# A list scheduler that makes its plan 48 times and keeps one, in a four-layer attention kernel

## The chip, the cores and the metric

One Trainium2 chip, one of its cores. The metric is device time in microseconds (us), lower is better. The engines are PE (matrix multiply; its weight loads are shown as PEld), DVE (vector), ACT (scalar and activation functions), POOL (GpSimd) and SP, whose queue issues the DMAs here. They run side by side, each in the order of its own instruction list, and wait for one another through semaphores.

## The reference

The input is x, 128 sequences of 64 tokens with 128 features, a context of the same shape and one conditioning vector per sequence, all float32. Four transformer layers follow one another. Cut to its blocks, in order:

```
L0: x = x + attn(adaln(x), adaln(ctx)) @ Wp
L1: x = x + gate * self_attn(adaln(x));  x = x + cross_attn(ln(x), ln(ctx))
    x = x + gate * gelu_mlp(adaln(x))
L2: x = x + gate * self_attn(adaln(x))
    x = x + gate * topk_cross_attn(adaln(x), ctx)      # softmax over the 16 largest of 64 scores
    x = x + gate * swiglu_mlp(adaln(x))
L3: x = x + gate * self_attn(adaln(x));  x = x + cross_attn(ln(x), ctx)
    x = x + gate * gelu_mlp(adaln(x))
```

Every attention has 16 heads of 8 features over 64 keys. There are seven attentions and three MLPs.

## The kernel before

**Tiling.** The 128 sequences are cut into 16 chunks of 8 sequences (512 tokens). A chunk goes through all four layers on its own. Eight lanes hold one chunk each; a lane whose list of work has become short takes the next chunk. So up to eight chunks, in different layers, are interleaved on the engines, and one fills the waits of another.

**The planner.** No order is written by hand. While the kernel is being built, on the host, `lane()` describes a chunk as operations: `op(engine, cost, outs, ins, give, latency)`. An operation is a group of instructions (for example the 64 matmuls that weigh the values of four sequences) with a hand-set weight in nanoseconds for the time it holds its engine, and a latency until its result can be used. `Plan.run` is a list scheduler: at each step it looks at the first 80 operations of each lane, asks `Plan.start` for the earliest time by the weights at which each could start (engine free, inputs ready, 150 ns for a hop between engines, 1300 ns for another activation table, a free tile, and for runs of small matmuls a term for the fetching of instructions, `late`), and gives out the one that can start first. `give_out` writes its instructions, and `in_turn` ties them to the previous ones of the same engine, so the chip executes each engine's list in the order of the plan. The weights set only this order: on the chip an instruction runs as soon as it is at the head of its engine's list and its inputs are there.

**Filling matmuls.** Where the plan finds that PE will stand idle for over 1000 ns before an operation that takes a fresh PSUM tile, `warm` (L1010 to L1018) puts dummy matmuls there into that tile, with columns for half the planned gap (`idle / 2`, at 1.7 ns a column). They are real instructions on the chip (L1017 in the profile). Their number of columns is thus a record of where the plan had gaps on PE, and how long.

**What the change touches.** In an attention, one operation makes the queries (PE, L586), ACT writes them to SBUF (L589), and then four DMAs spread them over a mask-shaped tile `qbd` whose other rows are zero, so that one matmul serves four heads. This transfer is the operation on SP at L595:

```
def spread():
    for j in range(4):
        nc.sync.dma_start(out=qbd()[j::4, j, :], in_=qT()[j::4, :])

op(SP, 1600, [qbd], [qT], spread, 2500)
```

The scores (L638, in the top-k attention L668) read `qbd`. ACT takes the exponentials (L649), PE weighs the values (L769), DVE divides (L778, L781), PE transposes (L816), ACT copies (L820), PE projects (L866). In the top-k attention, DVE finds the 16 largest scores of each row (L706, L708, L710, L721), and POOL masks (L736), ahead of transposes on PE (L744). A layer norm is DVE statistics (L530, L542), one POOL power (L545), DVE scaling (L550) and a PE transpose (L518). The gates of the residuals come from DRAM by DMAs on the same SP queue (L830). After the last chunk a small check (L1051 to L1061) decides whether a second, slow version of the whole network, which is also in the program, has to run; it does not run with these inputs.

Of the kernel before, what the change touches and what calls it, by code (L numbers as in the profile page):

```python
# [2 lines left out]

# [6 lines left out]
F32 = mybir.dt.float32  # L10
# [4 lines left out]
P = 128  # L15
# [4 lines left out]
T = CB * S  # L20
# [5 lines left out]
MLP = 512  # L26
LANES = 8
NJ = MLP // P
NSOME = 30
NQBD, NPROB, NVAL = 3, 8, 4  # L30
SCALE = 1.0 / math.sqrt(HD)
# [64 lines left out]
PE, DVE, ACT, POOL, SP = "PE", "DVE", "ACT", "POOL", "SP"  # L96


class Planned:


    def __init__(self, make, kind, turn):
        self.make, self.kind, self.turn = make, kind, turn
        self.real, self.writer, self.readers, self.ops, self.end = None, None, [], [], 0.0

    def __call__(self):
        if self.real is None:
# [4 lines left out]
class Operation:  # L112
    def __init__(self, engine, cost, latency, tiles, needs, give, bulk, table, small, within):
        self.engine, self.cost, self.latency = engine, cost, latency
        self.tiles, self.needs, self.give, self.bulk = tiles, needs, give, bulk
        self.table, self.small, self.within = table, small, within
        self.end = None


class Plan:  # L120

# [7 lines left out]
    BLOCK = 256  # L131
    FETCH = 3400.0

    def __init__(self, tc, slots, warm):
        self.tc, self.last, self.warm = tc, {}, warm
        self.size = slots
        self.free = {kind: [(0.0, k) for k in range(n)] for kind, n in slots.items()}
        self.made, self.next_turn = {}, {}
        self.engine_free = dict.fromkeys((PE, DVE, ACT, POOL, SP), 0.0)
        self.ops = None  # L140
        self.table = None
        self.small, self.blocks = 0, [(k, -self.FETCH) for k in range(0, self.BLOCK, 32)]
# [9 lines left out]

    def kept(self, real):
        t = Planned(None, None, None)
        t.real = real
        return t

    def op(self, engine, cost, outs, ins, give, latency=0.0, bulk=False, table=None, small=0, within=False):
        tiles = list(dict.fromkeys([*outs, *ins]))
        needs = {}  # L160
        for t in tiles:
            if t.writer is not None:
                needs[t.writer] = True
        for t in outs:
            needs.update(dict.fromkeys(t.readers))
        o = Operation(engine, cost, latency, tiles, needs, give, bulk, table, small, within)
        for t in outs:
            t.writer, t.readers = o, []
        for t in ins:
            if t not in outs:  # L170
                t.readers.append(o)
        for t in tiles:
            t.ops.append(o)
        self.ops.append(o)

    def start(self, o, first=True):
        at = self.engine_free[o.engine]
        if o.table not in (None, self.table):
            at += self.SWITCH
        if o.engine == PE and bool(o.small) != bool(self.small):  # L180
            at += self.SHAPE
        for d in o.needs:
            if d.end is None:
                return None
            at = max(at, d.end + (self.HOP if d.engine != o.engine else 0.0))
        want = {}
        for t in o.tiles:
            if t.real is None:
                want.setdefault(t.kind, []).append(t)
        o.want = want  # L190
        if want:
            if o.engine == PE:

                seen = {o}
                for t in o.tiles:
                    if t.kind in self.PSUM and t.real is None and not all(self.led(p, seen, want) for p in t.ops):
                        return None
            for kind, tiles in want.items():
                if len(self.free[kind]) < len(tiles) + (0 if first or kind != "some" else self.SPARE):
                    return None  # L200
                if tiles[0].turn is not None:
                    first = self.next_turn.get(kind, 0)
                    if sorted(t.turn for t in tiles) != list(range(first, first + len(tiles))):
                        return None
            for t in o.tiles:
                if t.real is None:
                    at = max(at, sorted(self.free[t.kind])[want[t.kind].index(t)][0])
        if o.small:
            at += self.late(o, at)
        return at  # L210
# [19 lines left out]
    def led(self, p, seen, want):  # L230

        if p.end is not None or p in seen:
            return True
        if not all(self.led(d, seen, want) for d in p.needs):
            return False
        seen.add(p)
        for t in p.tiles:
            if t.real is None and t not in want.setdefault(t.kind, []):
                want[t.kind].append(t)
        return True  # L240

    def give_out(self, o, at):
        idle, fresh = at - self.engine_free[o.engine], None
        for t in [t for tiles in o.want.values() for t in tiles]:
            if t.real is None:
                slots = self.free[t.kind]
                empty, t.slot = min(slots)
                slots.remove(min(slots))
                if o.engine == PE and t.kind in self.PSUM:
                    idle, fresh = min(idle, at - empty), fresh or t  # L250
                if t.turn is not None:
                    self.next_turn[t.kind] = t.turn + 1
                t()
        if fresh and idle > self.IDLE:
            self.in_turn(lambda: self.warm(fresh(), idle / 2))
        self.in_turn(o.give)
        self.table = o.table or self.table
        if o.engine == PE:
            self.small = o.small
            if o.small:  # L260
                self.late(o, at, True)
        self.engine_free[o.engine] = at + o.cost
        o.end = at + o.cost + o.latency
        for t in o.tiles:
            t.end = max(t.end, o.end)
            if t.kind is not None and all(p.end is not None for p in t.ops):
                self.free[t.kind].append((t.end + self.HOP, t.slot))
# [13 lines left out]

    def run(self, lanes, count):

        todo = [[] for _ in lanes]
        chunk = 0
        while True:
            for n, write in enumerate(lanes):
                if len(todo[n]) <= self.AHEAD and chunk < count:
                    self.ops = []
                    write(chunk)  # L290
                    todo[n] += [(chunk, o) for o in self.ops]
                    chunk += 1
            best = None
            oldest = min((c for ops in todo for c, _ in ops), default=None)
            for n, ops in enumerate(todo):
                for i, (c, o) in enumerate(ops[: self.WINDOW]):
                    at = self.start(o, c == oldest or o.within)
                    if at is not None and (best is None or (at, o.bulk, i, c) < best[0]):
                        best = (at, o.bulk, i, c), n, i, o
            if best is None:  # L300
                assert not any(todo), "no operation can start"
                return
            (at, *_), n, i, o = best
            del todo[n][i]
            self.give_out(o, at)
# [3 lines left out]
def kernel(ctx: ExitStack, tc: tile.TileContext, ins: dict, out: bass.AP, nchunk: int = NCHUNK):  # L309
# [33 lines left out]
    with tc.tile_pool(name="condw", bufs=1) as condw:  # L343
        cw = {}
        for key, wname, _, kinds in CONDS:
            n = len(kinds.split())
# [124 lines left out]
    def lane(n, plan, work, safe, acc, vblocks, queries, pool):  # L471
# [100 lines left out]
        def attention(hq, hkv, wq, bq, wk, wv, topk=False):  # L572
# [19 lines left out]
                for j in range(4):  # L592
                    nc.sync.dma_start(out=qbd()[j::4, j, :], in_=qT()[j::4, :])

            op(SP, 1600, [qbd], [qT], spread, 2500)  # L595


            pv = mm("pv")
# [410 lines left out]
    def network(lanes, safe, acc=None):  # L1009
        def warm(tile, ns):  # L1010
# [4 lines left out]
            while columns > 0:  # L1015
# [1 line left out]
                nc.tensor.matmul(flat[:, :n], lhsT=ident, rhs=W["L1_xcond_W_mlp1"][:, :n], start=True, stop=True)  # L1017
                columns -= n  # L1018

        plan = Plan(tc, {"mm": 3, "ps": 2, "po": 1, "qbd": 1 if safe else NQBD, "prob": 2 if safe else NPROB,  # L1020
                          "values": 1 if safe else NVAL, "some": 10 if safe else NSOME}, warm)
        with tc.tile_pool(name=f"work{int(safe)}", bufs=1) as work:


            vblocks = []
            for k in range(plan.size["values"]):
                v = work.tile([P, NPAIR, NH, 2, HW], F32, tag=f"vbuf{k}", name=f"vbuf{k}", bufs=1)
                nc.gpsimd.memset(v, 0.0)
                for b in range(2):
# [1 line left out]
                vblocks.append(v)  # L1031

            queries = []
            for k in range(plan.size["qbd"]):
                q = work.tile([P, 4, T], F32, tag=f"qbd{k}", name=f"qbd{k}", bufs=1)
                nc.gpsimd.memset(q, 0.0)
                queries.append(q)
            pool = [work.tile([P, T], F32, tag=f"some{k}", name=f"some{k}", bufs=1) for k in range(plan.size["some"])]
            plan.run([lane(n, plan, work, safe, acc, vblocks, queries, pool) for n in range(min(lanes, nchunk))], nchunk)
        return plan  # L1040

    acc = [const.tile([P, m], F32, name=k) for k, m in (("recsum", 4 * NH), ("fitting", 4 * NH), ("taken", 8))]
    fits = const.tile([P, 4 * NH], F32, name="fits")
# [45 lines left out]
```

## Time and profile before

| what | value |
|---|---|
| runs shown | 2002.7 us median (1995.64, 2002.7, 2008.0) |
| the profiled execution | 2011.3 us, its span 2009.5 us |
| PE, PEld, DVE, ACT, POOL busy, share of the span | 89%, 64%, 74%, 60%, 49% |
| mean granted PE clock | 0.977 of full speed |
| filling matmuls (L1017) on PE | 74.55 us in 220 records |
| weighing of the values (L769) on PE | 28672 matmuls, 314.2 us |
| exponentials (L649) on ACT | 384, 1025 ns each |
| `qbd` transfers (L593) on SP | 448, 64 KB each, 592 ns median issue, 1.9 us from issue to landing |
| gate transfers (L830) on SP | 448, 128 KB each, 616 ns median issue, 3.3 us to landing |

A busy time is the sum over an engine's instructions. A matmul of float32 data shows as two records. In the view by waits, each idle stretch of an engine is put down to what ended it; "issue" is idle time that ended without any release the profile shows. In the view by stretches of time, a column gives the busy us of each engine, the number of its instructions, and the clock granted to PE.

### The profile page before, as it was taken

What the parts mean: (1) busy time and instruction counts of PE and PEld (TensorE: products, weight loads), DVE (VectorE), ACT (ScalarE), POOL (GpSimd) and SP (SyncE); (2) the same over time, 40 slices, a digit from 0 to 9 for tenths busy, and PEclk for the clock granted to TensorE, in tenths of its full rate; (3) what the DMA queues carried; (4) which work ended last, traced back from release to release, by engine and by line L of the source; (5) the groups of instructions that cost most, each with busy time, mean ns of one, the idle gap of its engine ahead of it and who ended that gap; (6) DMA issues with size and microseconds to landing.
All of it is one profiled execution on the core that took longest, in us unless ns stands there. A gap on an engine that the chain in (4) does not pass through costs nothing. (4 is left out here: it accounts for less than half of the span.)

```text
span 2009.5 us, 104010 instructions
## 1 busy us (share of the span) xinstructions
PE 1791.5 (89%) x45345; PEld 1280.5 (64%) x45345; DVE 1488.3 (74%) x6641; ACT 1203.1 (60%) x1737; POOL 993.5 (49%) x1125
## 2 busy tenths in 40 slices
PE   4799889899899889999999988999898999888987
PEld 3466666666676666676676666676666666565564
DVE  3854546899989999787966496979588955989632
ACT  0356566675666657666665676677566665664443
POOL 2853534456455555555555355455454545444422
PEclk7899999999999999999999999999989999999999
DMA  5311222122122211222222222122112122121211
GB/s 173 88 51 51 66 62 66 54 58 73 57 68 63 69 51 53 69 83 66 65 67 66 64 73 63 51 68 66 56 55 61 45 71 61 56 65 31 66 31 35
DMA packets 203669, 127.51 MB, mean 63 GB/s; under 512 B 16764, under 2 KB 187972, under 8 KB 203204
## 3 DMA queue, kind: packets, MB, share of 16 engines
q1 hardware_dynamic: 196868, 115.44, 19.1%
q8 instruction: 359, 5.88, 1.2%
q10 hardware_dynamic: 6336, 5.31, 0.9%
q14 instruction: 106, 0.87, 0.2%
HBM read 86.22 MB, written 5.11 MB: 45 GB/s over the span
## 5 line engine op out<-in xcount | busy, mean ns | idle before, releaser
L649 ACT ACTIVATE prob<-ps 128x1024 f32<-128x1024 f32 x384 | 380.4, 1025 | 162.6 <-PE ps L638 161.7
L769 PEld LDWEIGHTS po<-vbuf,prob 128*32 128x32 f32 x28672 | 283.7, 110 | 140.4 <-issue 104.1
L769 PE MATMUL po<-vbuf,prob 128*32 128x18 f32 x28672 | 314.2, 187 | 54.0 <-issue 52.3
L545 POOL TENSOR_TENSOR rstd<-rstd,minus_half 128x4 f32<-128x4 f32 x192 | 200.3, 1046 | 154.9 <-DVE rstd L542 149.0
L736 POOL TENSOR_TENSOR some<-some,some 128x512 f32<-128x512 f32 x128 | 165.1, 1292 | 203.6 <-ACT some L728 199.7
L550 DVE TENSOR_SCALAR some<-x,parts,rstd 128x128 f32<-128x128 f32 x640 | 231.7, 425 | 44.6 <-POOL rstd L545 42.9
L638 PE MATMUL ps<-qbd,some 32*64 32x256 f32 x6144 | 238.0, 391 | 23.1 <-issue 18.1
L854 POOL TENSOR_TENSOR x<-x,some 128x512 f32<-128x512 f32 x112 | 143.9, 1286 | 208.5 <-DVE some L853 191.0
L708 DVE MATCH_REPLACE8 some<-m,some 128x64 f32<-128x64 f32 x1024 | 206.3, 209 | 0.0
L845 POOL TENSOR_TENSOR x<-x,some 128x512 f32<-128x512 f32 x112 | 145.6, 1300 | 104.9 <-DVE some L550 63.0
L778 DVE RECIPROCAL rec<-po 128x32 f32<-128x32 f32 x224 | 78.5, 350 | 154.6 <-PE po L769 149.0
L611 ACT COPY vbuf<-pv 64x512 f32<-64x512 f32 x224 | 139.0, 621 | 89.1 <-PE pv L604 86.9
L638 PEld LDWEIGHTS ps<-qbd,some 32*64 32x64 f32 x6144 | 122.8, 132 | 102.2 <-issue 66.4
L706 DVE MAX8 m<-some 128x8 f32<-128x64 f32 x1024 | 173.9, 211 | 9.8 <-ACT some L686 9.8
L710 DVE MAX8 m<-some 128x8 f32<-128x64 f32 x1024 | 176.8, 214 | 0.0
L853 DVE TENSOR_TENSOR some<-py,some 128x512 f32<-128x512 f32 x112 | 76.9, 687 | 121.0 <-PE py L879 50.0
L518 PE MATMUL pn<-ident,some 128*128 128x128 f32 x768 | 129.3, 286 | 31.4 <-issue 14.7
L582 ACT COPY some<-pk 128x512 f32<-128x512 f32 x112 | 66.0, 589 | 127.4 <-PE pk L580 120.4
L518 PEld LDWEIGHTS pn<-ident,some 128*128 128x128 f32 x768 | 90.0, 142 | 80.8 <-issue 32.3
L560 POOL TENSOR_TENSOR some<-some,mod_L 128x512 f32<-128x512 f32 x112 | 118.5, 1060 | 44.5 <-DVE some L559 40.0
L530 DVE BATCH_NORM_STATS2 parts<-x 128x6 f32<-128x256 f32 x320 | 121.0, 420 | 24.8 <-POOL x L854 16.1
L800 POOL TENSOR_SCALAR fits<-rec 128x64 f32<-128x64 f32 x112 | 42.7, 382 | 172.2 <-DVE rec L778 167.6
(219 smaller groups left out, 3632.7 us busy)
## 6 DMA issues: line engine op xcount, KB each, us to landing
some<-gates_dram SPq DMA_DIRECT2D x448, 128.0 KB, 3.3
qbd<-some SPq DMA_DIRECT2D x448, 64.0 KB, 1.9
some<-in_ctx_dram SPq DMA_DIRECT2D x64, 256.0 KB, 4.1
x<-in_x_dram SPq DMA_DIRECT2D x16, 256.0 KB, 4.6
out_dram<-x SPq DMA_DIRECT2D x16, 256.0 KB, 2.3
row<-in_biases_dram SPq DMA_DIRECT2D x17, 64.0 KB, 3.0
gates_dram<-gates SPq DMA_DIRECT2D x1, 896.0 KB
cw_L<-in_L_xcond_w_ada_dram ACTq DMA_DIRECT2D x1, 576.0 KB, 6.3
```

The source lines that it names most:

```text
L518: nc.tensor.transpose(p()[:, t * P : (t + 1) * P], x()[:, t, :], ident)
L545: op(POOL, 1070, [rstd], [rstd], lambda: nc.gpsimd.tensor_tensor(rstd(), rstd(), minus_half, ALU.pow))
L550: nc.vector.tensor_scalar(xn()[:, t, :], x()[:, t, :], mv()[:, t, 1:2], rstd()[:, t : t + 1], ALU.subtract, ALU.mult)
L638: nc.tensor.matmul(pscs[g // 2]()[b * S : (b + 1) * S, g % 2, u].rearrange("p (h q) -> p h q", h=4), lhsT=kT()[rows, cols], rhs=qbd()[rows ...
L649: op(ACT, 1020, [pr], [psc], lambda pr=pr, psc=psc: nc.scalar.activation(pr().rearrange("p g u h q -> p (g u h q)"), psc().rearrange("p g ...
L706: nc.vector.max(m1()[:, j, :], ex()[:, j, :])
L708: nc.vector.match_replace(w()[:, j, :], m1()[:, j, :], ex()[:, j, :], GONE)
L710: nc.vector.max(m2()[:, j, :], w()[:, j, :])
L736: op(POOL, 1310, [ex], [ex, w], lambda ex=ex, w=w: nc.gpsimd.tensor_tensor(ex(), ex(), w(), ALU.mult))
L769: nc.tensor.matmul(po()[32 * part : 32 * part + 32, h].rearrange("p b w -> p (b w)"), lhsT=prs[gp]()[:, gi, u, j, 32 * half : 32 * half + 32],
L845: op(POOL, 1310, [x], [x, g], lambda: nc.gpsimd.tensor_tensor(x(), x(), g(), ALU.add), bulk=True)
L854: op(POOL, 1310, [x], [x, y], lambda: nc.gpsimd.tensor_tensor(x(), x(), y(), ALU.add))
```

## The change

The planner is made able to run without writing instructions (`tc` is None), and somewhat faster by bookkeeping (`missing`, `ready`, `taken`). Each operation's weight is multiplied by a random factor between 0.99 and 1.01 from a seeded generator. The plan is made for seeds 0 to 47; the seed whose plan ends first by its own (varied) weights is then carried out. A plan that gets stuck counts as endless. The second, slow network takes seed 0. Separately, the weight of the mask transfer on SP goes from 1600 to 2900 ns, its latency stays 2500. No operation is added, removed or changed.

```diff
+TRIES = 48
 class Operation:
+        self.end, self.after = None, []
+        self.missing = sum(d.end is None for d in needs)
+        self.ready = 0.0
+        for d in needs:
+            d.after.append(self)
+            if d.end is not None:
+                self.ready = max(self.ready, d.end + (Plan.HOP if d.engine != engine else 0.0))
...
 class Plan:
-    def __init__(self, tc, slots, warm):
-        self.tc, self.last, self.warm = tc, {}, warm
+    def __init__(self, tc, slots, warm, seed):
+        self.tc, self.last, self.warm, self.random = tc, {}, warm, random.Random(seed)
...
-        o = Operation(engine, cost, latency, tiles, needs, give, bulk, table, small, within)
+        o = Operation(engine, cost * self.random.uniform(0.99, 1.01), latency, tiles, needs, give, bulk, table, small, within)
...
-        for d in o.needs:
-            if d.end is None:
-                return None
-            at = max(at, d.end + (self.HOP if d.engine != o.engine else 0.0))
+        at = max(at, o.ready)
...
-                t()
-        if fresh and idle > self.IDLE:
-            self.in_turn(lambda: self.warm(fresh(), idle / 2))
-        self.in_turn(o.give)
+                if self.tc is not None:
+                    t()
+        if self.tc is not None:
+            if fresh and idle > self.IDLE:
+                self.in_turn(lambda: self.warm(fresh(), idle / 2))
+            self.in_turn(o.give)
...
+                    if o.missing or best and max(o.ready, self.engine_free[o.engine]) > best[0][0]:
+                        continue
                     at = self.start(o, c == oldest or o.within)
...
-                assert not any(todo), "no operation can start"
-                return
+                return math.inf if any(todo) else max(self.engine_free.values())
...
-            op(SP, 1600, [qbd], [qT], spread, 2500)
+            op(SP, 2900, [qbd], [qT], spread, 2500)
...
+        def planned(seed, tc=None, work=None, *tiles):
+            plan = Plan(tc, slots, warm, seed)
+            tiles = tiles or (None, None, None)
+            return plan.run([lane(n, plan, work, safe, acc, *tiles) for n in range(min(lanes, nchunk))], nchunk)
+
+        seed = 0 if safe else min(range(TRIES), key=planned)
...
-            plan.run([lane(n, plan, work, safe, acc, vblocks, queries, pool) for n in range(min(lanes, nchunk))], nchunk)
-        return plan
+            assert planned(seed, tc, work, vblocks, queries, pool) < math.inf
```

More of the change, by code (lines that the diff above doesn't have):

```diff
@@ L1 @@
 import math
+import random
 from contextlib import ExitStack
@@ L104, in __init__ @@
         self.real, self.writer, self.readers, self.ops, self.end = None, None, [], [], 0.0
+        self.taken = False
     def __call__(self):
@@ L116, in __init__ @@
         self.table, self.small, self.within = table, small, within
-        self.end = None
+        self.end, self.after = None, []
[5 more added lines that the diff above has]
+                self.ready = max(self.ready, d.end + (Plan.HOP if d.engine != engine else 0.0))
 class Plan:
@@ L154, in kept @@
         t = Planned(None, None, None)
-        t.real = real
+        t.real, t.taken = real, True
         return t
@@ L181, in start @@
             at += self.SHAPE
-        for d in o.needs:
-            if d.end is None:
-                return None
-            at = max(at, d.end + (self.HOP if d.engine != o.engine else 0.0))
+        at = max(at, o.ready)
         want = {}
         for t in o.tiles:
-            if t.real is None:
+            if not t.taken:
                 want.setdefault(t.kind, []).append(t)
@@ L195, in start @@
                 for t in o.tiles:
-                    if t.kind in self.PSUM and t.real is None and not all(self.led(p, seen, want) for p in t.ops):
+                    if t.kind in self.PSUM and not t.taken and not all(self.led(p, seen, want) for p in t.ops):
                         return None
@@ L205, in start @@
             for t in o.tiles:
-                if t.real is None:
+                if not t.taken:
                     at = max(at, sorted(self.free[t.kind])[want[t.kind].index(t)][0])
@@ L237, in led @@
         for t in p.tiles:
-            if t.real is None and t not in want.setdefault(t.kind, []):
+            if not t.taken and t not in want.setdefault(t.kind, []):
                 want[t.kind].append(t)
@@ L244, in give_out @@
         for t in [t for tiles in o.want.values() for t in tiles]:
-            if t.real is None:
+            if not t.taken:
+                t.taken = True
                 slots = self.free[t.kind]
@@ L263, in give_out @@
         o.end = at + o.cost + o.latency
+        for d in o.after:
+            d.missing -= 1
+            d.ready = max(d.ready, o.end + (self.HOP if d.engine != o.engine else 0.0))
         for t in o.tiles:
@@ L293, in run @@
             best = None
-            oldest = min((c for ops in todo for c, _ in ops), default=None)
+            oldest = min((ops[0][0] for ops in todo if ops), default=None)
             for n, ops in enumerate(todo):
                 for i, (c, o) in enumerate(ops[: self.WINDOW]):
+                    if o.missing or best and max(o.ready, self.engine_free[o.engine]) > best[0][0]:
+                        continue
                     at = self.start(o, c == oldest or o.within)
@@ L1018, in warm @@
                 columns -= n
-        plan = Plan(tc, {"mm": 3, "ps": 2, "po": 1, "qbd": 1 if safe else NQBD, "prob": 2 if safe else NPROB,
-                          "values": 1 if safe else NVAL, "some": 10 if safe else NSOME}, warm)
+        slots = {"mm": 3, "ps": 2, "po": 1, "qbd": 1 if safe else NQBD, "prob": 2 if safe else NPROB,
+                 "values": 1 if safe else NVAL, "some": 10 if safe else NSOME}
+        def planned(seed, tc=None, work=None, *tiles):
[3 more added lines that the diff above has]
+        seed = 0 if safe else min(range(TRIES), key=planned)
         with tc.tile_pool(name=f"work{int(safe)}", bufs=1) as work:
             vblocks = []
-            for k in range(plan.size["values"]):
+            for k in range(slots["values"]):
                 v = work.tile([P, NPAIR, NH, 2, HW], F32, tag=f"vbuf{k}", name=f"vbuf{k}", bufs=1)
@@ L1033, in network @@
             queries = []
-            for k in range(plan.size["qbd"]):
+            for k in range(slots["qbd"]):
                 q = work.tile([P, 4, T], F32, tag=f"qbd{k}", name=f"qbd{k}", bufs=1)
@@ L1037, in network @@
                 queries.append(q)
-            pool = [work.tile([P, T], F32, tag=f"some{k}", name=f"some{k}", bufs=1) for k in range(plan.size["some"])]
-            plan.run([lane(n, plan, work, safe, acc, vblocks, queries, pool) for n in range(min(lanes, nchunk))], nchunk)
-        return plan
+            pool = [work.tile([P, T], F32, tag=f"some{k}", name=f"some{k}", bufs=1) for k in range(slots["some"])]
+            assert planned(seed, tc, work, vblocks, queries, pool) < math.inf
     acc = [const.tile([P, m], F32, name=k) for k, m in (("recsum", 4 * NH), ("fitting", 4 * NH), ("taken", 8))]
```

## The prediction

> **What bounds the kernel now.** I read the page first, then the view by stretches of time for the whole kernel, the same view for the filling matmuls alone (L1017), PE's waits, and three stretches closer.
>
> ```profile
> span 2009.5 us, 104010 instructions
> PE 1791.5 (89%) x45345; PEld 1280.5 (64%) x45345; DVE 1488.3 (74%) x6641; ACT 1203.1 (60%) x1737; POOL 993.5 (49%) x1125
> PE   4799889899899889999999988999898999888987
> ...
> DVE  3854546899989999787966496979588955989632
> ```
>
> PE is near full from the third slice to the last, DVE is full only in some slices. By stages (all engines, then L1017 alone):
>
> ```profile
> 0.00:100.00 100.00, 60.40 (x723) 40.41 (x723) 60.31 (x176) 20.86 (x29) 51.73 (x72) 0.83 0.45 131
> 100.00:1800.00 1700.00, 1555.45 (x41420) 1125.06 (x41421) 1308.80 (x5898) 1091.80 (x1577) 869.12 (x973) 0.99 0.21 62
> 1800.00:2009.50 209.50, 175.62 (x3204) 115.07 (x3204) 119.17 (x569) 90.41 (x132) 72.64 (x80) 0.97 0.14 40
> ```
>
> ```profile
> 0.00:100.00 100.00, 13.00 (x26) 5.72 (x26) 0.83 0.45 131
> 100.00:1800.00 1700.00, 23.76 (x86) 15.31 (x86) 0.99 0.21 62
> 1800.00:2009.50 209.50, 37.79 (x108) 18.93 (x108) 0.97 0.14 40
> ```
>
> First number after the length: PE busy. PE's own work is 1791.47 - 74.55 = 1716.9 us, and the change leaves every operation as it is, so only the rest of the span can move: 292.6 us of filling matmuls and idle PE. By stage that is 100 - 60.40 + 13.00 = 52.6 us at the start, 1700 - 1555.45 + 23.76 = 168.3 us in the middle and 209.5 - 175.62 + 37.79 = 71.7 us at the end.
>
> What the middle's idle time waits for on PE:
>
> ```profile
> PE po L769 <- issue: 51.8, 53, 2.1
> PE ps L638 <- issue: 18.1, 22, 2.0
> PE ps L668 <- issue: 10.7, 11, 2.3
> PE ppt L744 <- POOL some L736: 5.1, 6, 2.0
> PE pn L518 <- DVE some L550: 4.3, 7, 0.9
> ```
>
> Of the 144.55 us idle there, all "issue" waits come to 91 us, nearly all ahead of or inside the runs of small matmuls; waits for other engines are about 53.5 us in many small pieces. Three stretches show what the lanes' phases do to DVE:
>
> ```profile
> 400.00:700.00 300.00, 275.04 (x7212) 201.10 (x7215) 277.55 (x1402) 194.59 (x297) 165.68 (x179) 0.98 0.22 64
> 1600.00:1700.00 100.00, 93.96 (x2271) 67.45 (x2260) 51.54 (x136) 60.35 (x83) 50.14 (x62) 1.00 0.22 66
> 1790.00:1850.00 60.00, 50.82 (x1022) 34.13 (x1022) 58.07 (x367) 30.76 (x51) 25.43 (x27) 1.00 0.14 42
> ```
>
> Third busy number: DVE. It is 93% busy at 400 to 700, half idle at 1600 to 1700, and then 97% busy at 1790 to 1850, where the last top-k attentions come together and PE stops for them. After about 1940 one chunk is alone and PE waits at each link of its chain:
>
> ```profile
> 1986.66 2.54 PE L1017 MATMUL pn<-w_L_xcond_W_mlp,ident 128*128 128x512 f32 x6
> 1990.10 1.10 PE L518 MATMUL pn<-ident,some 128*128 128x128 f32 x4 [0.90 <-DVE some L550]
> ```
>
> So PE bounds the middle, DVE the stretch before the end, and one chunk's latency the end.
>
> **The change, part by part.** It changes only the order on each engine and the filling matmuls. I compared the two instruction lists. PE's are the same for some 70 matmuls and then differ nearly everywhere: this is another plan, not a retouched one.
>
> *Filling matmuls as a map of the plan's gaps.* Splitting the lists after 400 and 21,808 real matmuls (of 23,493 in the list; the second split is where the trace stands at 1800 us), the filling columns are 5,507 / 10,560 / 18,303 before and 5,697 / 12,392 / 13,169 after. Sums 34,370 and 31,258. So the new plan has shorter gaps at the end (-5,134), longer ones in the middle (+1,832), and the same start (+190).
>
> Price at the end: with all lost time put on the columns, 71.7 / 18.303 = 3.92 us per thousand; with the matmuls alone, 37.79 / 18.303 = 2.06. Ends of the range: -20.1 and -10.6 us. I take -20.1, since the two lines above show that filler and idle share each gap.
>
> Price in the middle: the matmuls alone 23.76 / 10.56 = 2.25 us per thousand, with the waits for engines (23.76 + 53.5) / 10.56 = 7.32. Ends: +4.1 and +13.4 us. No row tells which, as many waits lie where no filler stands; I take the half, +8.8.
>
> Start: 13.00 / 5.507 = 2.36 per thousand gives +0.4 (all lost time there: +1.8). I take +0.4.
>
> *Instruction waits of small matmuls (91 us).* They depend on how the runs follow each other. Of 223 steps from one run of L769 to the next, those with under 7 us of PE work from start to start are 153 before and 156 after (rows times their durations), so I take 0; ends -9 and +9, a tenth of the 91.
>
> On this the Trainium skill ("Runtime: NRT & Kernel Launch", Instruction fetch mechanics) says that instructions are fetched ahead in blocks of 256 and that the fetch is hidden, because a sequencer issues more slowly than the blocks arrive. The 53 waits ahead of L769 here speak against that for these runs, though the trace doesn't name their cause; by the rule the order could neither gain nor lose here, and the ends of this term would be 0.
>
> *Top-k work on DVE.* One of the 64 top-k groups costs DVE (206.3 + 176.8 + 173.9 + 83.6 + 96.2) / 64 = 11.5 us (rows L708, L710, L706, L708 loads, L721). In the last 3,000 real matmuls the new list has 8 groups against 12: 46 us of DVE work moved out of the 97% stretch into the earlier one where DVE is half idle. That is the reason behind the shorter gaps at the end, priced already. From 4,000 to 8,000 real matmuls (about 370 to 710 us) it has 20 groups against 16: 46 us more where DVE has 7% to spare. It is part of the longer gaps in the middle, and the rival below.
>
> *Table loads.* 70 against 72 on ACT before the end of the network, 1.28 us each, 2.6 us of an engine that is 60% busy: 0. If PE's cover were gone (the end), at most -2.6.
>
> *The mask's weight.* On the chip four issues take 2.4 to 2.5 us of SP in most cases, and a transfer lands 1.9 us after its issue, so qbd is complete about 1.8 + 1.9 = 3.7 us after the first issue (estimate from these rows). By the weights: 4.1 us before, 5.4 after; SP is held 1.6 before, 2.9 after. So the hold on SP is nearer than it was, the time to the result farther. In the middle PE waits for a qbd DMA once, 0.8 us, so little can be gained. The larger time makes the plan put other work ahead of the scores; the chip is not made to wait by that, except that in the last chunk alone two attentions could be put 1.3 us late: ends -0.8 and +2.6, I take 0. Behind a mask on SP stand mostly gate transfers (mask then gate 78 times before, 80 after), for which DVE L853 waits 46.9 us in all and POOL L845 27.1; both are waits off PE, so 0, unless they fall in the DVE-full stretch.
>
> *Sum.* -20.1 + 8.8 + 0.4 + 0 + 0 + 0 = -10.9 us. The profiled execution goes from 2011.3 (2009.5 of span and 1.8 around it) to 2000.4. It lay 8.6 us above the median shown; against the median, 2002.7 - 10.9 = 1991.8, so 1992 us. Within 1% means 1983 to 2023, about what a measurement can tell from no change.
>
> **Rivals.**
>
> *Slower: the top-k jam in the first wave.* The 46 us of added DVE work at 370 to 710 us meet about 25 us of idle DVE (7.5% of 340). 46 - 25 = 21 us don't fit, and PE, which needs the masked scores, ends the stretch 21 us later. If the end gives nothing back, because the last chunk's chain and not DVE sets it, the time is 2002.7 + 21 = 2024. For it: fillers between 4,000 and 6,000 real matmuls rise from 1,652 to 3,113 columns. Against: by 8,000 both lists have given out 23 groups, and other DVE work can move out. It decides against the change once the stretch grows by more than the end shrinks, 10.6 to 20.1 us.
>
> *Faster than 1%.* The plan's gain at the end (-20.1) comes whole, the middle costs only its fillers (+4.1) and the instruction waits fall by 9: -24.6, so 1978. For it: all gaps shorten together when the plan as a whole ends earlier. Against: 91 us of the waits are not the plan's to remove.
>
> *Nothing: the choice by weights doesn't carry over.* Variations of one per cent are smaller than the errors of the weights (the mask's own was off by half), so the chosen order is a random draw on the chip: 2003, plus or minus ten. Against: the fillers' places agree with the chip's gaps in the trace (108 of 220 records after 1800 us). The change not doing what it says is out: the lists differ and have fewer fillers.
>
> **How the numbers follow.** My forecast (small gain, 1983 to 2000) 0.35; nothing (1993 to 2013) 0.22; faster than 1% 0.26; the jam beyond 1% 0.17. Hence faster by over 1%: 0.26; within 1%: 0.35 + 0.22 = 0.57; slower by over 1%: 0.17. Range: low 1966, which is 1978 less the 7 us by which the lowest run lay under the median and less 5 for the unknown ends; high 2018, where most of the jam's case is left out. The likeliest case alone: 1983 to 2000.
>
> **What would show it.** In the changed profile: fillers (L1017) near 27 us after the end stage's start, 28 in the middle, 13 at the start; the stage after 21,808 real matmuls near 190 us instead of 209.5; DVE not full in the last stretch before one chunk is alone; the stretch from 370 to 710 us as long as before, to 9 us; "issue" waits of PE's small matmuls still near 91 us; PE's own work 1717 us. Wrong would be: a DVE at 97% or more around 400 to 750 us with PE waiting for L736 or L550; an end as long as before with fewer fillers but more idle; or issue waits that differ by more than 9 us.

## The result and the profile after

| | runs | median | lowest to highest |
|---|---|---|---|
| before | 18 | 2000.61 us | 1992.18 to 2010.68 |
| changed | 18 | 1989.4 us | 1982.45 to 1999.74 |

The ratio is 0.9948, 95% interval 0.9929 to 0.9966: 0.5% faster, clear of noise and within the 1%. The profiled execution of the changed kernel took 1987.86 us, its span 1986.1. In the changed kernel's code the line numbers are 16 higher: L1017 has become L1033, L769 is L785, L638 is L654, L853 is L869.

The page after, the same lines as before:

```profile
span 1986.1 us, 103877 instructions
PE 1784.4 (90%) x45327; PEld 1276.6 (64%) x45327; DVE 1495.9 (75%) x6641; ACT 1199.0 (60%) x1735; POOL 997.1 (50%) x1125
PE   4799899989988989999989899899999898988987
...
DVE  3854445999999999975777966499959977998632
```

PE still bounds. DVE is now at 90% or more in one long stretch, from the eighth to the seventeenth slice, and the two slices at 5 that stood ahead of the end (33 and 34) are now at 7. To set stage against stage, the cuts have to lie at the same real matmul (400 and 21,808 of the list), not at the same time. In the trace these stand at 104.8 and 1797.6 us before (the rows count records, two for a matmul of float32 data, so the 28672 of L769 in the table ahead are records too):

```profile
0.00:104.80 104.80, 65.20 (x763) 42.95 (x764) 65.08 (x184) 22.75 (x32) 55.95 (x76) 0.82 0.43 125
104.80:1797.60 1692.80, 1548.25 (x41251) 1120.36 (x41250) 1301.75 (x5879) 1087.51 (x1572) 864.90 (x970) 0.99 0.21 63
1797.60:2009.50 211.90, 178.02 (x3336) 117.23 (x3334) 121.45 (x581) 92.81 (x136) 72.64 (x80) 0.97 0.14 41
```

and at 103.4 and 1791.0 us after (all engines, then the fillers, L1033, alone):

```profile
0.00:103.40 103.40, 64.88 (x767) 42.71 (x771) 63.39 (x183) 22.70 (x31) 54.90 (x75) 0.85 0.44 126
103.40:1791.00 1687.60, 1553.96 (x41245) 1118.94 (x41248) 1333.02 (x6026) 1086.56 (x1579) 871.74 (x972) 0.99 0.21 62
1791.00:1986.10 195.10, 165.56 (x3330) 114.97 (x3326) 99.46 (x434) 89.74 (x127) 70.45 (x80) 0.95 0.15 46
```

```profile
0.00:103.40 103.40, 14.40 (x28) 6.20 (x28) 0.85 0.44 126
103.40:1791.00 1687.60, 27.65 (x94) 15.76 (x94) 0.99 0.21 62
1791.00:1986.10 195.10, 28.20 (x80) 14.68 (x80) 0.95 0.15 46
```

Lost time of PE is length less busy plus fillers. The fillers of the kernel before keep their 13.00, 23.76 and 37.79 us with these cuts.

| stage | lost before | lost after | difference | forecast |
|---|---|---|---|---|
| start | 52.6 | 52.9 | +0.3 | +0.4 |
| middle | 168.3 | 161.3 | -7.0 | +8.8 (4.1 to 13.4) |
| end | 71.7 | 57.7 | -14.0 | -20.1 (-20.1 to -10.6) |
| PE's own work | 1716.9 | 1714.2 | -2.8 | 0 |

The two profiles differ by 23.4 us, the medians by 11.2. The three chips of the experiments below ran the kernel before at medians of 2011, 2013 and 2014 us; its profile, at 2011.3, is like those, and the changed kernel's, at 1987.9, is like the result's runs. So about half of the 23.4 us isn't the change's, and nothing tells in which stages it lies. The -2.8 us in PE's own work say nothing of the change either: a second profile of the kernel before (at the end of the experiments) has 1714.0. Below, each kernel is compared with the kernel before on its own chip.

What PE's idle time waited for has changed as well. In the middle stage of the changed kernel the longest rows of the view by waits are:

```profile
PE po L785 <- issue: 52.4, 55, 2.2
PE ps L654 <- issue: 9.0, 12, 1.6
PE ppt L760 <- POOL some L752: 7.3, 9, 1.9
```

and in the end stage these, first before, then after:

```profile
PE ppt L744 <- POOL some L736: 6.4, 6, 1.9
PE po L769 <- issue: 0.5, 1, 0.5
```

```profile
PE po L785 <- issue: 9.1, 5, 2.6
```

After, the end stage has no row of waits for the masked scores (L752) any more. The table gives, before and after in us, the fillers, all "issue" rows added up, and the rest of PE's idle time, with the stretches too short to be listed:

| stage | fillers | "issue" idle | other idle |
|---|---|---|---|
| start | 13.0 to 14.4 | 14.7 to 14.2 | 24.9 to 24.3 |
| middle | 23.8 to 27.7 | 91.6 to 77.1 | 53.0 to 56.5 |
| end | 37.8 to 28.2 | 0.5 to 10.6 | 33.4 to 18.9 |

In the second profile of the kernel before the "issue" idle time is 14.0, 94.2 and 0.8 us, so what happened to it in the middle and at the end belongs to the order.

### The profile page after: what moved, and what is told of

The parts are those of the page before. It is cut to its first block, busy times and chain, and to the rows that moved or that the text cites. A ratio compares the mean times of both kernels' runs of the same rounds, so it can differ in the third digit from the quotient of the medians.

```text
span 1986.1 us, 103877 instructions
## 1 busy us (share of the span) xinstructions
PE 1784.4 (90%) x45327; PEld 1276.6 (64%) x45327; DVE 1495.9 (75%) x6641; ACT 1199.0 (60%) x1735; POOL 997.1 (50%) x1125
## 5 line engine op out<-in xcount | busy, mean ns | idle before, releaser
L785 PEld LDWEIGHTS po<-vbuf,prob 128*32 128x32 f32 x28672 | 283.3, 109 | 151.2 <-issue 117.9
L785 PE MATMUL po<-vbuf,prob 128*32 128x18 f32 x28672 | 315.7, 187 | 64.1 <-issue 62.2
L566 DVE TENSOR_SCALAR some<-x,parts,rstd 128x128 f32<-128x128 f32 x640 | 243.4, 443 | 31.2 <-POOL rstd L561 31.0
L752 POOL TENSOR_TENSOR some<-some,some 128x512 f32<-128x512 f32 x128 | 166.0, 1298 | 180.2 <-ACT some L744 176.9
L654 PE MATMUL ps<-qbd,some 32*64 32x256 f32 x6144 | 233.1, 395 | 13.4 <-issue 9.9
L654 PEld LDWEIGHTS ps<-qbd,some 32*64 32x64 f32 x6144 | 121.2, 133 | 86.1 <-issue 57.6
L869 DVE TENSOR_TENSOR some<-py,some 128x512 f32<-128x512 f32 x112 | 76.7, 685 | 78.9 <-PE py L895 41.8
```

Source lines behind the costliest of these rows:

```text
L566: nc.vector.tensor_scalar(xn()[:, t, :], x()[:, t, :], mv()[:, t, 1:2], rstd()[:, t : t + 1], ALU.subtract, ALU.mult)
L654: nc.tensor.matmul(pscs[g // 2]()[b * S : (b + 1) * S, g % 2, u].rearrange("p (h q) -> p h q", h=4), lhsT=kT()[rows, cols], rhs=qbd()[rows ...
L752: op(POOL, 1310, [ex], [ex, w], lambda ex=ex, w=w: nc.gpsimd.tensor_tensor(ex(), ex(), w(), ALU.mult))
L785: nc.tensor.matmul(po()[32 * part : 32 * part + 32, h].rearrange("p b w -> p (b w)"), lhsT=prs[gp]()[:, gi, u, j, 32 * half : 32 * half + 32],
```

## The experiments

The question is why it is faster, when the change alters only weights and their use. The planner returns, for each order, when it would end by its own weights. This is 1864.2 us for the kernel before, 1850.1 for the changed one (seed 25 of 48; 42 of the 48 end at all, the middle one at 1888.8 and the last at 1945.4). Two parts can be responsible, the choice and the mask weight. Theory A: an order is as good on the chip as by its weights. Theory B: an order is a draw. Theory C: the mask weight alone did it. The kernels name their seed outright; for a first plan it is the one that the search picks. The edits are against the changed kernel; long lines are cut to the part that changes, and a `+` line with a seed alone stands in place of the search.

**The mask weight alone** (one plan, nothing varied).

```diff
-cost * self.random.uniform(0.99, 1.01)
+cost * self.random.uniform(1.0, 1.0)
-        seed = 0 if safe else min(range(TRIES), key=planned)
+        seed = 0
```

> One part alone: the mask weight is 2900 and no weight is varied, one plan. By its weights this plan ends 33.5 us later (1897.7 us) than the plan of the kernel before (1864.2); the changed kernel's ends at 1850.1. Theory A (an order is as good on the chip as its end by the weights says, one for one): 2000.6 + 33.5 = 2034 us. Theory B (the choice doesn't carry over, an order is a draw): 2000 us, plus or minus 10. Theory C (the nearer mask weight is what made the changed kernel faster): 1989 us or less.

Measured: ratio 1.013 (1.0096 to 1.0164), 1.3% slower. Theory C falls. On the scale where the kernel before takes 2000.6 us it is 2026.6, 26 us up where the weights said 33.5.

**The choice alone** (mask weight 1600).

```diff
-            op(SP, 2900, [qbd], [qT], spread, 2500)
+            op(SP, 1600, [qbd], [qT], spread, 2500)
-        seed = 0 if safe else min(range(TRIES), key=planned)
+        seed = 0 if safe else 7
```

> The other part alone: the mask weight stays 1600, the best of seeds 0 to 47 by the weights (seed 7) is carried out. Its plan ends at 1839.4 us by the weights, 24.8 us ahead of the kernel before. Theory A: 2000.6 - 24.8 = 1976 us. Theory B: 2000 us, plus or minus 10. Theory C: no gain, about 2000 us.

Measured: ratio 0.9984 (0.9959 to 1.0009). Neither part alone gains: of the 24.8 us that the weights promised, 3 came, and the interval includes no gain at all. This stood against theory A. With the mask weight at 2900 the choice gave more: from the run before this one to the changed kernel 36 us (2026.6 to 1990.2), where the weights promised 47.6.

**The plan that ends last.**

```diff
+        seed = 0 if safe else 22
```

> The changed kernel, but of the 48 plans the one that ends last by its weights (of those that end: seed 22, 1945.4 us against 1850.1) is carried out. Theory A: 1989.4 + 95.3 = 2085 us. Theory B: 2000 us, plus or minus 10. If the chip follows the weights only in part, in between; the slope is what is read. Theory C says as theory B, but from 1989: the mask weight is the changed kernel's.

Measured: ratio 1.0374 (1.0326 to 1.0421), 2075 us on the common scale, against 2085 by theory A. Theory B falls: an order that the weights hold for bad is bad.

**The second of the 48.**

```diff
+        seed = 0 if safe else 46
```

> The changed kernel, but the second of its 48 plans (seed 46, ends at 1850.6 us by its weights, 0.5 us behind the first) is carried out. Theory A: 1990 us, and what it differs by is the scatter between orders that the weights hold for equal. Theory B: 2000 us, plus or minus 10. Theory C: 1989 us.

Measured: ratio 0.9845 (0.9812 to 0.9877), 1970 us: 20 us better than the changed kernel, at a plan only 0.5 us longer. This scatter between two orders that the weights hold for equal is about twice the whole gain of the change.

**The first of 300.**

```diff
+        seed = 0 if safe else 215
```

> The changed kernel with 300 seeds instead of 48: seed 215 ends first, at 1828.6 us by its weights, 21.5 us ahead of the changed kernel's plan. Put on the scale where the kernel before takes 2000.6 us, the first four orders stood 119 to 140 us above their plan where the mask weight is 2900. Theory A (the end by the weights carries over one for one, with a scatter of some 10 us): 1828.6 + 130 = 1959 us, ratio 0.979. Theory B' (the best of few is as good as it gets, a further search only finds plans that fit the weights and not the chip): no better than the changed kernel, 1990 us, ratio 0.995.

Measured: ratio 0.978 (0.9752 to 0.9808), 1957 us, theory A's forecast within 3 us. It beats both kernels. Its fillers, before and after 1800 us:

```profile
0.00:1800.00 1800.00, 38.47 (x110) 19.83 (x110) 0.98 0.23 67
1800.00:2100.00 300.00, 23.07 (x66) 11.67 (x66) 0.98 0.08 23
```

That is 61.54 us in all, against 70.25 in the changed kernel and 115.48 in the last of 48:

```profile
0.00:1800.00 1800.00, 67.34 (x198) 37.08 (x198) 0.98 0.22 64
1800.00:2100.00 300.00, 48.14 (x130) 22.89 (x130) 0.98 0.14 41
```

**A gate weight in place of the mask weight.** Why did the choice at 1600 give so little? In its trace DVE waits 51.3 us at L869 for gate transfers, which stand behind masks on SP; in the changed kernel 16.0. Theory D: the raised mask weight helps since it makes the plan count a truer load on SP.

```diff
-            op(SP, 2900, [qbd], [qT], spread, 2500)
+            op(SP, 1600, [qbd], [qT], spread, 2500)
-            op(SP, 200, [g], behind, fetch, 4000)
+            op(SP, 1300, [g], behind, fetch, 4000)
+        seed = 0 if safe else 9
```

> The mask weight stays 1600, and the gate transfers' weight on SP goes from 200 to 1300 ns (two issues of 616 ns are about 1.25 us), latency as it was; the first of 48 seeds by these weights (seed 9, 1834.5 us). Theory D (what helped in the raised mask weight is that the plan counts a truer load of SP's queue, so that gate transfers queued behind masks are not planned too early): DVE waits for gate transfers, 49 and 52 us in the two runs at 1600 and 200, fall to 20 us or less, and the time stands 119 to 140 us above the plan as in the runs at 2900: 1954 to 1975 us, ratio 0.977 to 0.987. Theory E (it is the mask itself that matters): the waits stay near 50 us and the time stands 158 us above the plan as in the choice alone: 1992 us, ratio 0.996.

Measured: ratio 0.9917 (0.9885 to 0.9948), 1984 us, 149 above its plan. The waits did as theory D said, the time did not. DVE's waits for gates, in the choice alone, in the changed kernel and here:

```profile
DVE some L869 <- DMA some<-gates_dram: 51.3, 19, 6.6
```

```profile
DVE some L869 <- DMA some<-gates_dram: 16.0, 8, 5.9
```

```profile
DVE some L869 <- DMA some<-gates_dram: 2.5, 5, 0.7
```

Nearly 50 us of waits went, and the order stands 149 us above its plan, where the kernel before, with 46.9 us of such waits, stands 136 above its own. Theory D's time (1954 to 1975) lies outside the interval (1978 to 1990), so it falls as it was put. That these waits lie off the path is the likely reading; one order can't show it alone, as equal orders differ by up to 20 us.

**The second of the 48 at 1600.**

```diff
-            op(SP, 2900, [qbd], [qT], spread, 2500)
+            op(SP, 1600, [qbd], [qT], spread, 2500)
+        seed = 0 if safe else 13
```

> Mask weight 1600, gate weight 200, as in the choice alone, but the second of its 48 plans (seed 13, 1843.6 us by the weights). Theory D: this order too holds DVE up for gate transfers (40 us or more) and stands about 150 us above its plan: 1994 us, ratio 0.997. Theory F (the choice alone had bad luck, the scatter between orders that the weights hold for equal): 130 us above its plan, 1974 us, ratio 0.987.

Measured: ratio 0.9955 (0.9934 to 0.9975), 1992 us, 148 above its plan; DVE's gate waits are 19.4 us. So the choice alone had not merely bad luck, and gate waits are again not the reason.

**The first of 300 at 1600.**

```diff
-            op(SP, 2900, [qbd], [qT], spread, 2500)
+            op(SP, 1600, [qbd], [qT], spread, 2500)
+        seed = 0 if safe else 156
```

> Mask weight 1600, the first of 300 seeds (seed 156, 1830.4 us by the weights), the partner of the first of 300 at 2900 (1828.6 by the weights, ratio 0.978). Theory G (with the mask weighed too short, a plan is put together tighter than the chip can carry out): like the other orders at 1600 it stands about 148 us above its plan, 1978 us on the scale where the kernel before takes 2000.6, ratio 0.989. Theory F (both weights are as good, what differed so far was scatter): 129 us above, 1959 us, ratio 0.979.

Measured: ratio 0.9933 (0.9904 to 0.9962), 1987 us, 157 above its plan. Searching six times as many orders gained 10 us at this weight and 34 us at 2900; by the weights it promised 9.0 and 21.5, so this alone doesn't speak against the search at 1600.

**The middle of the 48 at 2900.**

```diff
+        seed = 0 if safe else 2
```

> The changed kernel, but a plan from the middle of its 48 (seed 2, 1888.8 us by the weights). Theory A, one for one at 129 us above the plan: 2018 us, ratio 1.009. Theory B (an order is a draw): 2000 us, ratio 1.000, plus or minus 0.005. A chosen order would then gain 1.4% by the choice among 48, against the middle one.

Measured: ratio 1.0168 (1.0132 to 1.0204), 2034 us, 145 above its plan. So the choice among 48 is worth 2.2% against the middle one of the same weights (0.9948 / 1.0168 = 0.978).

**The middle of the 48 at 1600.**

```diff
-            op(SP, 2900, [qbd], [qT], spread, 2500)
+            op(SP, 1600, [qbd], [qT], spread, 2500)
+        seed = 0 if safe else 2
```

> Mask weight 1600, a plan from the middle of its 48 (seed 2, 1884.2 us by the weights). Theory G: 148 us above its plan, 2032 us, ratio 1.016. Theory F: as the middle plan at 2900, 129 us above its own, 2013 us, ratio 1.006.

Measured: ratio 1.0352 (1.0304 to 1.04), 2071 us, 187 above its plan, more than either theory gave. PE's waits for masks in the kernel before, the changed one, and this one:

```profile
PE ps L638 <- DMA qbd<-some: 1.8, 3, 0.8
```

```profile
PE ps L654 <- DMA qbd<-some: 1.4, 2, 1.0
```

```profile
PE ps L654 <- DMA qbd<-some: 12.8, 9, 2.8
```

**The kernel before again**, unchanged, for a second profile:

> The kernel before, unchanged, for a second profile: how far two executions of one order differ stage by stage. If the stages (start, middle, end) repeat to about 3 us, the stage differences between the two kernels shown so far can be read as they stand; if the middle moves by 10 us, they can't.

Measured: 2011.71 us. Its stages, cut at the same matmuls:

```profile
0.00:102.40 102.40, 63.04 (x764) 41.94 (x765) 63.55 (x183) 22.18 (x31) 54.53 (x75) 0.85 0.43 128
102.40:1797.80 1695.40, 1547.76 (x41250) 1118.30 (x41249) 1303.73 (x5880) 1088.46 (x1572) 868.29 (x971) 0.99 0.21 62
1797.80:2009.80 212.00, 176.75 (x3336) 116.51 (x3334) 121.55 (x581) 92.89 (x136) 72.72 (x80) 0.98 0.14 40
```

They repeat to 2.6 us, the end to 0.1. But these two executions have nearly the same total, so they don't show where the 12 us lie that the profiles of the two kernels differ by beyond their medians. The end is 16.8 us shorter after (195.1 against 211.9), more than all of these 12 us, so at least a part of that is the order's; the middle's -7.0 is not settled.

**All orders together.** Times are the ratio times 2000.6 us.

| order | mask weight | by its weights | on the chip | above the plan |
|---|---|---|---|---|
| first of 300 | 2900 | 1828.6 | 1956.6 | 128 |
| changed kernel, first of 48 | 2900 | 1850.1 | 1990.2 | 140 |
| second of 48 | 2900 | 1850.6 | 1969.6 | 119 |
| middle of 48 | 2900 | 1888.8 | 2034.2 | 145 |
| not varied | 2900 | 1897.7 | 2026.6 | 129 |
| last of 48 | 2900 | 1945.4 | 2075.4 | 130 |
| first of 300 | 1600 | 1830.4 | 1987.2 | 157 |
| first of 48 | 1600 | 1839.4 | 1997.4 | 158 |
| second of 48 | 1600 | 1843.6 | 1991.6 | 148 |
| kernel before, not varied | 1600 | 1864.2 | 2000.6 | 136 |
| middle of 48 | 1600 | 1884.2 | 2071.0 | 187 |

At 2900 a line through the six orders rises 1.03 us on the chip for each us of plan (correlation 0.98, standard error of the slope 0.11), with 9 us of scatter. So theory A holds there, to that scatter. At 1600 the orders stand 157 us above their plans on the mean, at 2900 132; the difference, 25 us, is 2.7 times its standard error (scatter 19 over five orders, 9 over six). So the orders made with the mask weight of 2900 stand nearer to their plans. What that is worth in time is less clear: of five pairs of the same rank, four are faster at 2900 (by 7, 22, 31 and 37 us) and the pair that isn't varied is slower by 26, 14 us faster on the mean with a standard error of 11. One order can't show it, as the kernel before happened to be the luckiest of its group (136). That the plan's end is also a better guide at 2900 (a scatter of 9 us against 19) hangs on two of the five orders at 1600 and is not shown.

What the plans at 1600 leave out isn't settled. Most likely it is not the gate waits. PE's own waits for masks are longer at 1600 (1.8, 2.3 in its repetition, 3.0, 3.2, 8.8 and 12.8 us over both kinds of scores, and 4.4 with the raised gate weight, against 1.0 to 2.2 at 2900), which has the right sign and is too small for 25 us.

**No fillers**, the changed kernel's order:

```diff
-    IDLE = 1000.0
+    IDLE = 1e9
+        seed = 0 if safe else 25
```

> The changed kernel's plan with no filling matmul at all (they compute nothing; the order of everything else is the same). They take 70.25 us of PE. If they only stand in gaps and the clock holds without them: the 27.65 us of the middle are partly given back, 1975 to 1989 us. If they hold the granted clock up in the gaps: the clock falls below 0.977 and the time rises above 1990 us.

Measured: ratio 1.006 (1.0033 to 1.0088), so 1.1% slower than the changed kernel (1.006 / 0.9948); the granted clock is 0.956 against 0.977. The column before the last two is the clock:

```profile
0.00:100.00 100.00, 52.31 (x715) 36.91 (x715) 60.11 (x176) 21.18 (x29) 52.58 (x73) 0.78 0.46 131
100.00:1800.00 1700.00, 1536.74 (x40939) 1103.74 (x40924) 1317.23 (x5925) 1078.72 (x1559) 866.00 (x967) 0.98 0.21 62
1800.00:2019.70 219.70, 169.47 (x3487) 119.80 (x3486) 116.99 (x542) 102.72 (x147) 78.95 (x87) 0.88 0.15 45
```

The end runs at 0.88 instead of 0.95 to 0.96, and PE's own work takes 1758.5 us (the sum of the three busy times) against 1714.2. The 70 us of fillers cost less than they save. The Trainium skill ("TensorE: Matmul & The Clock Gate", Part 1: The HAM clock gate) says that the array's default is the throttled clock and that activity releases it; these rows agree.

## Why the prediction was right, point by point

**The total.** Forecast 2002.7 - 10.9 = 1992 us; measured 1989.4, against a median before of 2000.61: -11.2 us. The sum came out right. That it did so within 3 us is in part luck: the second of the 48 has fillers of nearly the same length (69.4 us for 70.25) and takes 20 us less, so a forecast from fillers carries at least that much scatter. And in the two profiles the lost time fell by 20.6 us, not 10.9, with an unknown part of this the executions' own.

**The fillers as a map of the gaps.** Fillers per stage were forecast at 13, 28 and 27 us and are 14.40, 27.65 and 28.20: right. Over the orders the sum of the fillers ranks those of one mask weight, each time with one exchange. At 2900 fillers of 61.5, 69.4, 70.25, 87.6, 100.1 and 115.5 us go with 1957, 1970, 1990, 2034, 2027 and 2075 us; at 1600 fillers of 57.5, 60.2, 67.1, 74.55 and 79.5 us go with 1987, 1997, 1992, 2001 and 2071. Across the two weights it doesn't hold: 57.5 us at 1600 stand for 1987 us, 61.5 at 2900 for 1957.

**The end.** -14.0 us of lost time for -20.1, inside the two bounds (-20.1 and -10.6). It is made of two parts that the forecast didn't tell apart. The fillers fell by 9.6 us and the idle time other than "issue" by 14.4: together -24.0, even more than the price with all lost time on the columns. Against that, 10.1 us of new "issue" idle time appeared, nearly all ahead of L785. The reason given for the shorter gaps fits: DVE, 58.07 us busy of 60 at 1790 to 1850 before, is 51.25 there now, and 76.14 instead of 51.54 at 1600 to 1700, and PE's 6.4 us of waits for masked scores in the end stage are gone.

**The middle.** +8.8 forecast, -7.0 measured. The gaps went as forecast: fillers +3.9 us (the low price said +4.1), other idle time +3.5, together 7.4 and inside the ends (+4.1 and +13.4). What turned the sign is the "issue" idle time, 91.6 to 77.1 us, that is -14.5; it fell ahead of the scores (L638, 18.1 to 9.0 us) and not ahead of the runs of L769.

**Issue waits, taken as 0 with ends of 9 us.** This is the term that failed. In the middle, where its 91 us were read, it measured -14.5, outside the ends, and so did one of the signs of being wrong (issue waits that differ by more than 9 us) come true. At the end, where the forecast had none, it measured +10.1. The count of short steps between the runs of L769 (153 and 156) foretold neither. Over the whole span the two nearly cancel, 106.8 to 101.8 us, and that is why it did little harm to the sum. So the order does move these waits, also against the argument that they are not the plan's to remove; what causes them no run here shows. Ends of 0, which the prediction worked out beside its own, would have been further off still. In the orders at 2900 the sum goes from 99.7 to 111.6 us, higher in the slower ones, but this is little beside the 119 us between them.

**Top-k jam in the first wave.** Did not happen to the extent feared. From 4,000 to 8,000 real matmuls the kernel before needs 322.3 us, the changed one 329.6: 7 us longer, not 21. DVE's added work found room, at 94% busy (the changed kernel's row):

```profile
356.10:685.70 329.60, 303.10 (x7671) 216.52 (x7670) 310.73 (x1614) 217.95 (x329) 182.81 (x192) 0.99 0.20 60
```

**The mask's weight, taken as 0.** Right for the waits it named (PE for qbd 1.4 us after 1.8; and removing nearly all of DVE's gate waits in the run with the gate weight brought nothing that shows). What it left out: the weight also decides which of 48 orders is taken. Without a choice the raised weight costs 26 us, with it the orders of the same rank are 7 to 37 us faster.

**The rival "nothing".** It said that variations of 1% are smaller than the errors of the weights, so the choice is a draw. The premise is true and the conclusion false: the variations shake the order, and the weights, wrong as they are, put the six orders at 2900 in their place within 9 us. For this change alone the rival came close all the same: its 10 us are of the size of that scatter.

## What to carry to other kernels

A list scheduler is a gamble whose result moves by several per cent when its weights move by one; making many plans and keeping the one that ends first carries over to the chip as far as the weights are honest, here one for one at a scatter of 9 us with the mask weight at 2900, and a longer search (300 plans) gave 2.2% against the kernel before. The orders made with the nearer mask weight stood 25 us closer to their plans, so it may pay to mend the weights before searching, though the reason wasn't found here and a raised gate weight in one order showed no such thing. Judge a changed weight over several orders, never by one. Where a kernel fills planned gaps with dummy work, their sum ranks the orders of one set of weights before anything runs, to some 20 us here. And compare idle time stage by stage and by what ended it: a term that is small over the whole span can hide two large ones of opposite sign.

## What the runs showed of the hardware

The kernel before differs by 0.5 to 0.7% in its median between groups of runs (2000.6 us in the result's, and 2011, 2013 and 2014 us on the three chips of the experiments), as much as this change brings, while the stages of one order repeat to 2.6 us between two executions of nearly the same total. Leaving out 70 us of work that computes nothing made PE's own work 44 us longer (1758.5 against 1714.2 us, at a mean granted clock of 0.956 against 0.977). Idle time of PE that no release in the profile explains depends on the order of the work: between two orders of the same operations it moved by -14.5 us in one stage and +10.1 in another, and between two executions of one order by at most 2.6.
